# A graph layer on Trainium2: a mark on GpSimd ahead of every gather

## The chip, the cores and the metric

The kernel runs on one core of one Trainium2 chip. Its engines are called as in the profile: PE is TensorE (PEld its weight loads), DVE is VectorE, ACT is ScalarE, POOL is GpSimd and SP is SyncE. The metric is the device time of one execution in microseconds (us), and the lower the better. Times before are the median of three runs; the profile comes from one execution of its own, which has its own time.

## The reference

One layer of a graph transformer over 6250 nodes of 256 features in f32. It adds to the input x an attention over the edges (64 output features, 4 heads), a linear attention over all nodes, and then a mixture of experts (8 experts, the best 2 of them for each node). The part that this case is about is the attention over the edges:

```python
xn = _layernorm(x)
h = xn @ W                                 # 6250 x 64
el = h @ Wl.T;  er = h @ Wr.T              # 6250 x 4 heads each
e = exp(leaky_relu(el[src] + er[dst], 0.2))          # one row for each edge
rowsum = segment_sum(e, src, 6250)
w = e / maximum(rowsum, 1e-12)[src]
heads = [segment_sum(w[:, hd:hd+1] * h[dst], src, 6250) for hd in range(4)]
gnn = elu(stack(heads, axis=1) + b).reshape(6250, 256)
x = x + gnn + linear_attention(xn)
x = x + experts(_layernorm(x))
```

There are 206,250 edges: 100,000 in both directions and a loop on every node. They come sorted by dst, and the sums run over src, so the kernel sorts them by src. For every edge it needs the row of its dst node: `er` (4 numbers) and `h` (64 numbers).

## The kernel before, in words

**Tiles.** The 6250 nodes are 49 tiles of 128. First come the projections (`project`), and beside them the first pass of the sort (`sort_batch`), which drops every edge into a grid by pairs of src tiles. `project` also stores `table` in the chip's memory: one row of 69 f32 for each node, with `er`, `h` and a one.

**A block's edges.** `pack(q)` (L835) takes the pair q of src tiles, places its edges into 36 columns of 128 for each tile (35 of them used), and leaves two things: `dst_x` (L907, three buffers), the row numbers in `table`, and `loc` (L916), the place of each edge's src node in its tile. For each tile of the pair it then calls `gather`.

**The gather.** `gather` (L924) takes the buffer `xe` (three of them), 128 partitions by 35 columns by 69 f32, and issues 35 indirect DMAs from POOL (L927), one for each column: 128 rows of `table` chosen by one column of `dst_x`. 49 blocks of 35 gathers are 1715. They run on eight DMA semaphores in turn, so that a gather carries a wait for the one eight ahead of it. The first gather of a block waits besides for `dst_x` (DVE) and for the free `xe` buffer, which is free when the sums of the block three ahead of it (PE, `a_ps` at L996) have read it. From the first gather on POOL has no other work.

**What reads them.** `look(b, k)` (L935) builds the one-hot matrix `oh` of block b (L939), transposes it on PE (`t_ps`, L952), copies it with ACT (`ohT`, L956) and multiplies it with `elw` to give each edge its src part of the weight (`e_ps`, L964). `weights` (L971) adds up the three parts (L973), adds the gathered `er` (L977: the first reader of `xe`), takes the leaky relu and ACT's exponential, and puts the result in a PSUM bank. `sums` (L984) multiplies `oh` by the weights (`ohw`, L989, DVE) and sums the rows of `xe` on PE (`a_ps`, L996), with one matmul for each column. `xe` is the operand that is loaded as weights there, 65 columns wide, and the heads come out by `heads` (L789).

**The order.** The loop over blocks runs in program order, with `look` for the next block and `pack` for a pair two ahead put between the four steps of `sums`. Each step also runs a piece of other work with `some_more`: first the linear attention (`attention`, L543), then the experts of tiles that are done (`finish_steps`, L629; its matmuls are L739 and L755). Within an engine the instructions are in the order in which they were written; the engines meet through semaphores that the framework adds from the reads and writes of tiles. The loads and stores of x and of the output are issued from SP, and the gathers alone from POOL.

Of the kernel before, what the change touches and what calls it, by code (L numbers as in the profile page):

```python
# [34 lines left out]
def tile_gps_layer(  # L35
# [22 lines left out]
    nc = tc.nc  # L58
# [776 lines left out]
    def pack(q):  # L835
# [78 lines left out]
        for u in range(min(U, NT - q * U)):  # L914

            loc = gw.tile([P, GC, S, 2], BF16, name="loc", bufs=5)  # L916
            for i in range(S):
                nc.vector.scalar_tensor_tensor(
                    loc[:, :, i], lo[:, u, i * CS:i * CS + GC, None].to_broadcast([P, GC, 2]),
                    float(-u * P), lack[:, :, i], op0=OP.add, op1=OP.subtract,  # L920
                )
            ready[q * U + u] = (gather(dst_x[:, u * CW:u * CW + CPT]), loc)

    def gather(dst_x):  # L924
        xe = gw.tile([P, CPT, TW], F32, name="xe", bufs=3)
        for c in range(CPT):
            nc.gpsimd.indirect_dma_start(  # L927
                out=xe[:, c, :],
                out_offset=None,
                in_=table,  # L930
                in_offset=bass.IndirectOffsetOnAxis(ap=dst_x[:, c:c + 1], axis=0),
            )
        return xe

    def look(b, k):  # L935
# [252 lines left out]
```

## Time and profile before

| what | value |
|---|---|
| median of 3 runs | 4406.96 us (4391.23 to 4422.44) |
| profiled execution | 4420.71 us, of it span 4418.9 us |
| mean clock granted to TensorE | 0.694 |
| busy: PE / PEld | 2317.2 us / 1665.5 us |
| busy: DVE / ACT | 1975.3 us / 710.3 us |
| busy: POOL | 1678.3 us, of it gathers (L927) 1630.0 us in 1715 |
| software DMA queue (q0) | 54880 packets, 60.70 MB |

The span is the time between the first and the last instruction of the profiled execution, and 1.8 us lie around it. "Busy" is the time in which an engine works on an instruction; waits, semaphore instructions and the issuing of DMAs are not in it, apart from the gathers[...]. A line such as `L927` is a line of the kernel. In the profile's groups the columns are: line, engine, operation, output <- inputs, count; busy time and mean ns of one; idle time of the engine ahead of them, and what ended most of it. "remote" or "another core or an unknown queue" means that the profile found nothing that released the instruction. A list of durations such as `938/944/947` is the least, the median and the largest in ns. POOLq is the sequencer of POOL: the semaphore instructions stand under it.

The first gather starts at 459.9 us and the last at 4255.4 us. The gathers come in bursts of 35, one for each block.

### The profile page before, as it was taken

Reading aid. Unit: us, or ns where it says so; the run is one execution under the profiler, and the core shown is the slowest. Engines: PE = TensorE matmul, PEld = TensorE weight load, DVE = VectorE, ACT = ScalarE, POOL = GpSimd, SP = SyncE. Lnnn points to the kernel's source line nnn. Section 1 sums busy time; section 2 is a strip of 40 time slices with the busy share of each in tenths; the row PEclk is TensorE's granted clock in tenths of the full one; section 3 lists DMA queues with packets and bytes.
Section 4 is the critical chain, followed back from the end, with each engine's and each line's share of the span. In section 5 each row is a group of like instructions: output and inputs, shape, how many; then the busy total and the mean of one; then the engine's idle time right before and its main releaser. Section 6 shows DMA issues by size and latency. Waiting matters only on the chain.

```text
span 4418.9 us, 39444 instructions
## 1 busy us (share of the span) xinstructions
PE 2317.2 (52%) x15347; PEld 1665.5 (38%) x15347; DVE 1975.3 (45%) x4111; ACT 710.3 (16%) x1465; POOL 1678.3 (38%) x1779
## 2 busy tenths in 40 slices
PE   7876234333436554574645463464364463553658
PEld 4544123223324433352533342343243242342446
DVE  7889425443543443352543343244144253333443
ACT  4543001011101111111111110110110110110123
POOL 1001653445452433514343523523524435344220
PEclk8766556656657776696877675686686586685779
DMA  1120111111130101101100101100101101011010
GB/s 56 32 23 1 32 21 33 36 36 40 30 75 12 28 13 20 26 17 17 25 17 19 26 10 19 28 11 18 26 12 26 18 17 24 15 21 22 12 18 8
DMA packets 106677, 103.92 MB, mean 24 GB/s; under 512 B 42726, under 2 KB 78788, under 8 KB 106484
## 3 DMA queue, kind: packets, MB, share of 16 engines
q0 software_dynamic: 54880, 60.70, 8.0%
q1 hardware_dynamic: 49908, 39.75, 3.2%
q8 instruction: 122, 2.00, 0.2%
q10 hardware_dynamic: 1696, 0.89, 0.1%
q14 instruction: 71, 0.58, 0.0%
HBM read 86.57 MB, written 14.65 MB: 23 GB/s over the span
## 4 chain that ended last, share of the span: by engine, by line
another core or an unknown queue 37%; PE 24%; DVE 15%; issue 10%; ACT 4%; POOL 1%; DMA 0%; DVEq 0%; ACTq 0%; POOLq 0%
PE a_ps L996 8%; PE h_ps L739 6%; PE y_ps L755 6%; DVE rc L889 4%; DVE ohp L894 4%; DVE ohc L882 2%; PE y_ps L730 1%; POOL xe L927 1%; PE y_ps L679 1%; DVE ohw L989 1%; ACT ohT L956 1%; ACT hT L747 1%; DVE inc L853 1%; ACT L747 1%
## 5 line engine op out<-in xcount | busy, mean ns | idle before, releaser
L927 POOL DMA_INDIRECT xe<-table,dst_x x1715 | 1630.0, 950 | 2266.2 <-PE a_ps L996 1566.6
L996 PE MATMUL a_ps<-ohw,xe 128*65 128x128 f32 x4410 | 627.8, 298 | 302.3 <-issue 223.0
L996 PEld LDWEIGHTS a_ps<-ohw,xe 128*65 128x65 f32 x4410 | 563.4, 154 | 360.6 <-issue 262.7
L989 DVE TENSOR_TENSOR ohw<-oh,bank 128x1280 f32<-128x1280 bf16 x196 | 323.6, 1652 | 597.4 <-remote 514.3
L739 PE MATMUL h_ps<-tokT,w1s 128*128 128x512 f32 (+2 forms) x896 | 454.0, 625 | 79.5 <-ACT hT L747 58.4
L755 PE MATMUL y_ps<-w2s,hT 128*128 128x256 f32 x1568 | 438.8, 418 | 76.3 <-issue 71.6
L899 PE MATMUL s_ps<-rc,ohp 128*128 128x144 f16 x2525 | 267.4, 282 | 255.0 <-DVE ohp L894 202.9
L759 DVE SCALAR_TENSOR_TENSOR x<-y_ps,comb,x 128x256 f32<-128x256 f32 x392 | 189.6, 484 | 416.6 <-PE y_ps L755 295.6
L755 PEld LDWEIGHTS y_ps<-w2s,hT 128*128 128x128 f32 x1568 | 309.8, 208 | 172.4 <-issue 116.8
L964 PE MATMUL e_ps<-elw,ohT 128*128 128x48 bf16 x588 | 35.6, 198 | 623.7 <-ACT ohT L956 594.5
L899 PEld LDWEIGHTS <-ohp 128*128 128x128 f16 x2525 | 233.1, 125 | 319.9 <-DVE ohp L894 249.0
L747 ACT ACTIVATE hT<-h_ps,b1s 128x512 f32<-128x512 f32 (+2 forms) x224 | 142.0, 634 | 885.0 <-PE h_ps L739 404.6
L964 PEld LDWEIGHTS <-ohT 128*128 128x128 bf16 x588 | 28.7, 105 | 657.6 <-ACT ohT L956 614.7
L889 DVE TENSOR_TENSOR rc<-ohc,bank 128x1152 f16<-128x1152 f16 (+1 forms) x350 | 227.7, 695 | 57.5 <-remote 49.6
L956 ACT COPY ohT<-t_ps 128x768 bf16<-128x768 bf16 x98 | 78.2, 798 | 1070.0 <-remote 858.6
L739 PEld LDWEIGHTS h_ps<-tokT,w1s 128*128 128x128 f32 x896 | 172.6, 217 | 187.0 <-issue 95.3
L731 DVE TENSOR_TENSOR x<-x,y_ps 128x256 f32<-128x256 f32 x49 | 20.6, 421 | 404.0 <-PE y_ps L730 384.7
L894 DVE TENSOR_TENSOR ohp<-to,bank 128x2048 f16<-128x2048 f16 (+1 forms) x175 | 195.4, 1116 | 0.0
L853 DVE TENSOR_TENSOR_SCAN inc<-ones,t_ps 128x404 f32<-128x404 f32 x50 | 49.7, 993 | 284.4 <-remote 222.5
L567 PE MATMUL y_ps<-cw,qT 128*128 128x256 f32 x98 | 49.4, 599 | 203.7 <-ACT qT L565 89.2
L730 PE MATMUL y_ps<-b2s,cTs 8*128 8x256 f32 x98 | 55.4, 663 | 134.0 <-ACT cTs L728 134.0
L567 PEld LDWEIGHTS y_ps<-cw,qT 128*128 128x128 f32 x98 | 21.9, 273 | 272.5 <-ACT qT L565 161.9
(266 smaller groups left out, 2756.9 us busy)
## 6 DMA issues: line engine op xcount, KB each, us to landing
xe<-table,dst_x POOLq DMA_INDIRECT x1715
xt<-in_x_dram SPq DMA_DIRECT2D x24, 512.0 KB
base_y<-xt SPq DMA_DIRECT2D x12, 512.0 KB
yt<-base_y SPq DMA_DIRECT2D x11, 512.0 KB
out_dram<-x SPq DMA_DIRECT2D x11, 512.0 KB
w1s<-in_L_ffn_w_dram SPq DMA_DIRECT2D x8, 256.0 KB
w2s<-in_L_ffn_w_dram SPq DMA_DIRECT2D x8, 256.0 KB
table<-tab SPq DMA_DIRECT2D x12, 138.0 KB
```

Source lines behind the costliest of these rows:

```text
L730: nc.tensor.matmul(yb, lhsT=cTs, rhs=b2s, start=True, stop=True)
L739: nc.tensor.matmul(h_ps[:, :w], lhsT=w1s[:, e, c, f * P:(f + 1) * P], rhs=held["tokT"][:, c, :w], start=(c == 0), stop=(c == DC - 1),)
L747: nc.scalar.activation(held[e][:, f, :w], h_ps[:, :w], AF.Gelu, bias=b1s[:, k:k + 1])
L755: nc.tensor.matmul(y_ps, lhsT=held[e][:, f, j * P:(j + 1) * P], rhs=w2s[:, e, f, :], start=(f == 0), stop=(f == FC - 1),)
L759: nc.vector.scalar_tensor_tensor(x2[:, j, :], y_ps, held["comb"][:, j, e:e + 1], x2[:, j, :], op0=OP.mult, op1=OP.add,)
L889: nc.vector.tensor_tensor(pairs(rc[:, :m, i, :]), pairs(ohc[:, :m]), twos(edges_q[:, t0:t0 + m, i, :], U * CW // 2), op=OP.mult,)
L894: nc.vector.tensor_tensor(pairs(ohp[:, :m]), twos(to[:, 1, t0:t0 + m], P // 2), iota_2.to_broadcast([P, m, P // 2, 2]), op=OP.is_equal,)
L899: nc.tensor.matmul(flat(s_ps), lhsT=ohp[:, t - t0, :], rhs=flat(rc[:, t - t0]), start=(t == 0), stop=(t == NBT - 1),)
L927: nc.gpsimd.indirect_dma_start(out=xe[:, c, :], out_offset=None, in_=table, in_offset=bass.IndirectOffsetOnAxis(ap=dst_x[:, c:c + 1], axis=0),
L956: nc.scalar.copy(ohT, t_ps)
L989: nc.vector.tensor_tensor(ohw[:, :n], oh[:, g0:g1, i, None, :].to_broadcast([P, n, H, SN]), ew_s[:, c0:c0 + n, :, None].to_broadcast([P, n ...
L996: nc.tensor.matmul(a_ps[:, i].rearrange("f h n -> f (h n)"), lhsT=xe[:, c, H:], rhs=ohw[:, c - c0].rearrange("p h n -> p (h n)"), start=(c ...
```

## The change

`gather` calls a new function `in_turn` for each of its DMAs. It puts an instruction that does nothing (`nop`, the mark) on POOL ahead of the gather. Two dependences without a semaphore keep the order: the mark behind the gather before, and the gather behind its own mark. A dependence with a semaphore makes the gather wait for the mark of the gather ahead of it, across blocks too. The very first gather has no such wait. In the built program each mark is one semaphore instruction on POOL that raises a semaphore of POOL's own. A gather waits for one semaphore: where it was the DMA semaphore of the gather eight ahead, it is now the mark's, and the wait for the DMA semaphore is a semaphore instruction of its own between the mark and the gather. POOL has 1927 instructions before and 5334 after, with 1717 DMAs in both.

```diff
@@ -921,15 +921,36 @@
+    issued = []
+    marks = []
+
+    def behind(ins, other, by):
+        tc.add_manual_dep(
+            ins.ins, other.ins.name, mybir.DependencyInfo(by, mybir.DependencyReason.DATA)
+        )
+
+    def in_turn(issue):
+
+
+        mark = nc.gpsimd.nop()
+        if issued:
+            behind(mark, issued[-1], mybir.DependencyClass.NoSync)
+        row = issue()
+        behind(row, mark, mybir.DependencyClass.NoSync)
+        if marks:
+            behind(row, marks[-1], mybir.DependencyClass.Sync)
+        marks.append(mark)
+        issued.append(row)
+
     def gather(dst_x):
         xe = gw.tile([P, CPT, TW], F32, name="xe", bufs=3)
         for c in range(CPT):
-            nc.gpsimd.indirect_dma_start(
+            in_turn(lambda: nc.gpsimd.indirect_dma_start(
                 out=xe[:, c, :],
                 out_offset=None,
                 in_=table,
                 in_offset=bass.IndirectOffsetOnAxis(ap=dst_x[:, c:c + 1], axis=0),
-            )
+            ))
         return xe
```

## The prediction

> **What bounds the kernel now.** I read the page's busy row first, then the chain that ended last, then the groups of the changed line, and last the trace around one block's gathers, by windows.
>
> ```profile
> PE 2317.2 (52%) x15347; PEld 1665.5 (38%) x15347; DVE 1975.3 (45%) x4111; ACT 710.3 (16%) x1465; POOL 1678.3 (38%) x1779
> another core or an unknown queue 37%; PE 24%; DVE 15%; issue 10%; ACT 4%; POOL 1%; DMA 0%; DVEq 0%; ACTq 0%; POOLq 0%
> L927 POOL DMA_INDIRECT xe<-table,dst_x x1715 | 1630.0, 950 | 2266.2 <-PE a_ps L996 1566.6
> L956 ACT COPY ohT<-t_ps 128x768 bf16<-128x768 bf16 x98 | 78.2, 798 | 1070.0 <-remote 858.6
> ```
>
> No engine is full, and 37% of the chain is put down to something the profile can't name: 0.37 x 4418.9 = 1635 us. POOL's share of the chain is 1%, so the gathers look like no bound. The windows say otherwise. These are 48 us before a burst of 35 gathers (one block's) and the 43 us from 6.5 us after its start:
>
> ```profile
> core 0: us, PE busy (x) PEld busy (x) DVE busy (x) ACT busy (x) POOL busy (x), PEclk, DMA share, GB/s
> 2570.00:2618.00 48.00, 45.09 (x283) 31.57 (x281) 40.85 (x86) 9.99 (x15) 0.00 (x0) 1.00 0.00 1
> 2625.00:2668.00 43.00, 5.18 (x34) 3.70 (x33) 3.99 (x4) 0.06 (x1) 28.00 (x30) 0.59 0.16 26
> ```
>
> PE goes from 45 busy us in 48 to 5 in 43. The chain over the same place, and the gathers there:
>
> ```profile
> 2620.13 0.69 ACT hT L747
> 2620.81 47.10 another core or an unknown queue
> 2667.94 0.81 ACT ohT L956
> ```
>
> ```profile
> L927 POOL DMA_INDIRECT xe<-table,dst_x x35: 938/944/947, 2618.5 to 2660.9; - x35
> L927 POOLq EVENT_SEMAPHORE  x2: 43/38638/77232, 2537.8 to 2654.6; - x2
>   issue: 10.1, 33
> ```
>
> The last gather ends at 2661.84; ACT resumes 6.1 us later. The trace has the semaphore updates of PE's matmuls that were issued ahead of the stall arriving one by one through the burst. So while POOL issues gathers, PE's completions come late and everything that hangs on them stands. Why, the trace doesn't show. The same picture is at most of the 49 bursts, with ACT waits of 47.0 to 47.1 us at 1461, 1626, 2288, 2942, 3260, 3577, 3895 and 4215. As data the gathers are early (block 14's end at 1502.2, their reader, the add into z at L977, runs at 1622.4); only block 0's are waited for directly. Hence the rule for the sum: **a burst that gets longer by d moves the end by about d**, for some 42 of the 49 bursts; 42 is the count in this row, where POOL found PE's release before it:
>
> ```profile
> POOL xe L927 <- PE a_ps L996: 1566.6, 42, 82.9
> ACT ohT L956 <- remote: 858.6, 34, 47.1
> ```
>
> Here page and trace disagree. The Trainium skill, SBUF — State Buffer, section "SBUF: two separate sides", says engine ports and DMA ports are disjoint, so that a DMA and a compute operation don't slow each other. By that rule a burst longer by 5 us costs nothing (the data has 36 to 120 us to spare); by the windows above it costs about 42 x 5 = 210 us. I take the windows.
>
> **The change, part by part.** The instruction order on PE, DVE, ACT, SP and POOL stays as it was; there are 1715 gathers before and after, the same DMAs. Added on POOL's queue are 3407 semaphore instructions: 1715 marks, and about 1692 separate waits. A gather of before carries one wait, that the gather eight ahead of it has landed. After, it carries the wait for the mark, and the wait for the landing stands as an instruction of its own ahead of it.
>
> The gather itself: 0.944 us (median of the row) and a constant gap of 0.30 us (10.1 us of issue over 33), so a cadence of 1.249 us and 35 x 1.249 - 0.30 = 43.4 us a burst. The first eight gathers of the program carry no landing wait and have the same gap, so a satisfied wait on a gather costs nothing there. The new wait is for the mark ahead of the *previous* gather, which POOL's sequencer has executed before it ever reaches this gather: always satisfied, **0**. Behind a gather on POOL stand only later gathers; their readers are L977 and L996's weight loads.
>
> The marks and separate waits: the nearest row is the EVENT_SEMAPHORE of L927, 43 ns when satisfied; the one place with two in a row (458.894 and 458.981) has them 87 ns apart. Two for each gather: 87 to 174 ns of the sequencer's time, 150 to 300 us over the kernel if nothing hid it. The cover is that the sequencer runs ahead. In the burst above, the semaphore instruction of the *next* block is at 2654.6, just before gather 29 of 35 starts (2654.65): six gathers were already handed over and waiting. So the sequencer made 35 gathers in 2654.65 - 2618.47 = 36.2 us, at most 1.03 us each, and since it meets the start of a gather to 0.1 us it was being held by a full queue and needs less. Even 1.03 + 0.174 = 1.21 us is under the cadence of 1.249. The ends: **0** (all hidden) and 0.174 x 35 x 42 = **256 us** (all exposed). I take 0, because the row shows the sequencer six ahead, and keep 256 for the range.
>
> A rule speaks against this. Advanced Engine Details and Errata, section "Network/Comms", gives 50 to 100 ns for reading a semaphore from a sequencer on trn2: 100 to 200 ns for two a gather, an estimate of 42 x 35 x (0.1 to 0.2) = 147 to 294 us if it were on the path. The trace has 43 to 87 ns and the run-ahead; by these the sum is 0.
>
> The moved wait: the landing wait now holds the sequencer, not the queue. Packets start 1.64 us after a gather's issue and have landed 2.1 to 2.7 us after it; the gather eight later is due 8 x 1.249 = 9.99 us after. 7.3 us to spare, **0**. The run-ahead may shrink; one gather ahead is enough.
>
> At the first gather of a block, the mark and waits are passed while the sequencer still waits for dst_x (the 77.2 us instruction at 2537.8), and the gather then starts 0.26 us after PE's release, as before. If they came after the release instead: 42 x 0.087 to 0.174 = 4 to 7 us. I take **+4**. Code: the skill's Runtime: NRT & Kernel Launch, section "Instruction fetch mechanics", has 256 instructions in 16 KiB, so 64 B each; 3407 are 218 KB, an estimate of 27 more packets of the size that the instruction queue q14 shows (0.58 MB in 71, 8 KB). Ends: 0 and 27 x 2.1 us (a gather's landing as the nearest transfer) = 57 us. Before, POOL's 1927 instructions needed some 15 such packets and no gap of 0.30 inside a burst shows one; two exposed is my choice, **+4**.
>
> **Sum** against the profiled execution: 4420.7 + 4 + 4 = 4429. That execution lies 14 us over the median of the runs shown, 4407; on the median's footing the forecast is **4415**. A measurement of this kernel tells about 1% from no change: 4363 to 4451.
>
> **Rivals.**
> A, slower: the sequencer isn't far enough ahead once it has three instructions for one. It decides from the point where mark, wait and gather together take over 1.249 us of the sequencer, or where marks fill queue places so that the run-ahead runs dry. For: at most 1.03 us is known today, so as little as 0.05 us more than I count puts it over; 30 ns a gather is already 35 x 42 x 0.03 = 44 us, 1%. Against: the alignment to a full queue. Price: one instruction exposed 0.087 x 35 x 42 = 128 us, 4543; both 256 us, 4671.
>
> B, slower by code: pages exposed one after another, 57 us, 4472. Against: fetching ahead was invisible so far; for: three times as many in the same bursts.
>
> C, faster: what delays PE in the bursts is eased. For: 1635 us of the chain are unexplained; the stall starts 4 to 12 us into a burst, when the sequencer is at the gathers whose wait names one of the same burst, and the change takes that wait off the gathers. Against: the stall outlasts the last gather by 6 us, when no gather waits, and PE's matmuls at L899 in the first bursts, which wait for no gather, are late too. A tenth of 1635 us is 164 us: 4251.
>
> That the change does nothing that counts is the forecast itself, as its wait is always satisfied.
>
> **How the numbers follow.** Forecast (hidden) 0.40, A 0.26, B 0.10, C 0.24. So faster by over 1% 0.24, within 1% 0.40, slower 0.36. The forecast's own range is 4385 to 4440. The range is 4290 to 4600: it holds the forecast, B, A with one instruction exposed, and the smaller half of C; the far half of C (0.12) and A with both exposed (0.08) are left out.
>
> **What would show it.** Right: gathers of 0.944 us with a gap of 0.30, bursts of 43.4 us, some 3450 EVENT_SEMAPHORE on the gathers' lines, ACT waits of 47 us unchanged, the chain's unknown share at 37%. A: the gap between gathers grows to 0.39 or 0.48 and the ACT waits to 50 or 53 us, the next block's semaphore instruction moves to the burst's end. B: single gaps of about 2 us, up to 27 of them. C: the same cadence, yet PE busy well over 5 us in the 43, and shorter ACT waits. Wrong altogether if the gathers themselves change their 0.944 us.

## The result, and the profile after

The changed kernel takes **4538.93 us** (median of 4 runs, 4530.64 to 4543.47) against 4402.57 us of the kernel before in the same comparison: a ratio of 1.031, 95% interval 1.0277 to 1.0343. It is slower by 3%, some 136 us. The profiled execution has a span of 4537.6 us against 4418.9, which is 118.7 us more at nearly the same granted clock (0.691 against 0.694).

From the page of the changed kernel: the busy row, the chain's shares, the gathers' group, and the queue that brings instructions.

```profile
PE 2378.6 (52%) x15347; PEld 1700.8 (37%) x15347; DVE 1974.3 (44%) x4111; ACT 709.8 (16%) x1465; POOL 1681.0 (37%) x1779
...
another core or an unknown queue 35%; PE 22%; DVE 15%; issue 13%; ACT 3%; POOL 2%; DMA 1%; POOLq 1%; DVEq 0%; ACTq 0%
...
L948 POOL DMA_INDIRECT xe<-table,dst_x x1715 | 1632.5, 952 | 2386.3 <-POOLq L935 1593.1
```

```profile
q14 instruction: 98, 0.80, 0.1%
```

The gathers are busy as long as before (1632.5 us against 1630.0). q14 brings 98 packets instead of 71, exactly the 27 that the prediction counted. The lines of the gathers and of the marks by themselves, with the least, median and largest duration in ns:

```profile
L948 POOLq EVENT_SEMAPHORE  x1744: 2/17/119346, 335.2 to 4371.4; - x194
L948 POOL DMA_INDIRECT xe<-table,dst_x x1715: 939/947/1928, 455.6 to 4373.7; - x191
```

```profile
L935 POOLq EVENT_SEMAPHORE  x1714: 2/17/1397, 11.5 to 4368.6; - x191
```

The two lines have 3458 semaphore instructions, and they take POOL's sequencer 17 ns in the median. Some 50 of them are the waits at the head of a block, which stood there before (51 on L927). So POOL does nearly what was expected of it: its gap between two gathers is still 0.305 us in the median.

Where are the 119 us? Worked out from the starts and ends of the gathers: the 49 bursts last 2173.0 us in all, before 2137.7 (+35.3); the time between bursts is 1746.0 us, before 1658.8 (+87.2); what lies ahead of the first burst and behind the last is 4 us less. **Three quarters of the loss lie where no gather runs.** One pair of bursts shows how. These are windows of before, a burst (44 us) and the stretch up to the next burst:

```profile
3325.00:3369.00 44.00, 8.40 (x70) 6.35 (x68) 7.90 (x15) 1.38 (x2) 33.01 (x35) 0.63 0.16 32
3369.00:3407.00 38.00, 20.33 (x164) 17.78 (x164) 30.72 (x58) 2.39 (x6) 0.42 (x1) 0.58 0.02 2
```

And the same two of after (columns: window, length, busy us of PE, PE's weight loads, DVE, ACT and POOL with counts, clock, share of the DMA engines, GB/s):

```profile
3413.00:3457.00 44.00, 5.39 (x52) 5.15 (x52) 2.52 (x6) 0.21 (x1) 32.95 (x35) 0.59 0.15 28
3457.00:3501.00 44.00, 23.53 (x178) 19.54 (x178) 35.38 (x67) 3.15 (x7) 0.37 (x1) 0.56 0.02 1
```

The burst is the same for POOL: 35 gathers, 33 us busy. PE gets 52 matmuls through in it instead of 70, and DVE does 6 operations instead of 15. The work that did not fit comes after the burst, and the stretch grows from 38 to 44 us. Over all bursts, 3817 of PE's matmuls start inside them before, and 3394 after. Counted by the gather beside which they start, the loss is at one place: beside the sixth to tenth gather of a burst PE starts 1103 matmuls before and 560 after. Ahead of that it is 1691 and 1647, and from the eleventh gather on there are even more after (1187 against 1023).

The granted clock hardly moved: over the bursts 0.643 before and 0.639 after, between them 0.730 and 0.724. But the matmuls moved within it. From the first burst on, 3689 of them start while the clock is at half, before 3335, and PE's busy time is 61 us more for the same 15347 matmuls. How much of the loss comes in this way and how much by later starts is not shown.

The other 35 us are single gaps in some bursts: 30 gaps over 0.4 us, together 32.6 us over the usual one. The gathers at the end of the seventh burst:

```profile
897.13 0.94 POOL L948 DMA_INDIRECT xe<-table,dst_x  x1 [0.33 <-issue]
899.94 0.95 POOL L948 DMA_INDIRECT xe<-table,dst_x  x1 [1.86 <-DMA xe<-table,dst_x]
902.04 0.95 POOL L948 DMA_INDIRECT xe<-table,dst_x  x1 [1.16 <-issue]
904.84 0.95 POOL L948 DMA_INDIRECT xe<-table,dst_x  x1 [1.85 <-DMA xe<-table,dst_x]
```

In the trace the marks and waits around them take 0.69 to 0.71 us each instead of 17 ns, and some twice that. 574 of POOL's semaphore instructions are that slow, half of them behind position 28 of a burst and hardly any ahead of 20 outside the first four bursts. PE's semaphore updates in the bursts mostly arrive at multiples of about 0.70 us, before as after (2.80, 2.13, 3.52, 5.60 us in the burst at 2618 of before). Of 236 steps of over 0.35 us between such updates, from 7 us into a burst on, 202 lie within 0.08 us of a multiple before, and 111 of 131 after. Two engines with the same step of 0.7 us suggested the first theory: in a burst, the sequencers of all engines get something in turns of 0.7 us.

### The profile page after: what moved, and what is told of

Same layout as the page of the kernel before. It is cut to its first block, busy times and chain, and to the rows that moved or that the text cites. A ratio compares the mean times of both kernels' runs of the same rounds, so it can differ in the third digit from the quotient of the medians.

```text
span 4537.6 us, 42851 instructions
## 1 busy us (share of the span) xinstructions
PE 2378.6 (52%) x15347; PEld 1700.8 (37%) x15347; DVE 1974.3 (44%) x4111; ACT 709.8 (16%) x1465; POOL 1681.0 (37%) x1779
## 4 chain that ended last, share of the span: by engine, by line
another core or an unknown queue 35%; PE 22%; DVE 15%; issue 13%; ACT 3%; POOL 2%; DMA 1%; POOLq 1%; DVEq 0%; ACTq 0%
PE a_ps L1017 7%; PE h_ps L739 6%; PE y_ps L755 6%; DVE rc L889 4%; DVE ohp L894 3%; DVE ohc L882 2%; POOL xe L948 2%; PE y_ps L730 1%; DVE ohw L1010 1%; DVE inc L853 1%; ACT ohT L977 1%; DMA xe<-table,dst_x 1%; ACT hT L747 1%; DVE x L759 1%
## 5 line engine op out<-in xcount | busy, mean ns | idle before, releaser
L948 POOL DMA_INDIRECT xe<-table,dst_x x1715 | 1632.5, 952 | 2386.3 <-POOLq L935 1593.1
L1017 PE MATMUL a_ps<-ohw,xe 128*65 128x128 f32 x4410 | 666.7, 307 | 366.0 <-issue 334.3
L1017 PEld LDWEIGHTS a_ps<-ohw,xe 128*65 128x65 f32 x4410 | 591.5, 159 | 442.5 <-issue 395.3
L739 PE MATMUL h_ps<-tokT,w1s 128*128 128x512 f32 (+2 forms) x896 | 476.2, 647 | 179.5 <-ACT hT L747 110.4
L1010 DVE TENSOR_TENSOR ohw<-oh,bank 128x1280 f32<-128x1280 bf16 x196 | 322.8, 1647 | 550.8 <-remote 528.1
L882 DVE TENSOR_TENSOR ohc<-to,bank 128x1152 f16<-128x1152 f16 (+1 forms) x175 | 120.0, 686 | 0.4 <-ACT to L871 0.4
L426 DVE TENSOR_TENSOR ohp<-rank,iota_h 128x4096 f16<-128x4096 f16 (+1 forms) x51 | 115.7, 2269 | 2.8 <-ACT rank L419 2.6
```

The source lines that it names most:

```text
L739: nc.tensor.matmul(h_ps[:, :w], lhsT=w1s[:, e, c, f * P:(f + 1) * P], rhs=held["tokT"][:, c, :w], start=(c == 0), stop=(c == DC - 1),)
L882: nc.vector.tensor_tensor(pairs(ohc[:, :m]), twos(to[:, 0, t0:t0 + m], U * CW // 2), iota_2[:, :, :U * CW // 2].to_broadcast([P, m, U * CW ...
L948: in_turn(lambda: nc.gpsimd.indirect_dma_start(out=xe[:, c, :], out_offset=None, in_=table, in_offset=bass.IndirectOffsetOnAxis(ap=dst_x[: ...
L1010: nc.vector.tensor_tensor(ohw[:, :n], oh[:, g0:g1, i, None, :].to_broadcast([P, n, H, SN]), ew_s[:, c0:c0 + n, :, None].to_broadcast([P, n ...
L1017: nc.tensor.matmul(a_ps[:, i].rearrange("f h n -> f (h n)"), lhsT=xe[:, c, H:], rhs=ohw[:, c - c0].rearrange("p h n -> p (h n)"), start=(c ...
```

## The experiments

Each ratio is against runs of the kernel before on the same chip. Their medians differ by chip (4411.9 us for the first four, 4363.95 for the next four, 4408.99 for the last two), so the spans of different groups are not compared to one per cent.

**One of the two added instructions, or both without the moved wait.** The theories at the start were the turns, a store of instructions ahead of POOL's sequencer that runs out, and the landing wait that was moved from the gather's queue into the sequencer.

```diff
-        mark = nc.gpsimd.nop()
-        if issued:
-            behind(mark, issued[-1], NoSync)
+        if len(issued) < 8:
+            issued.append(issue())
+            return
+        wait = nc.gpsimd.nop()
+        behind(wait, issued[-1], NoSync)
+        behind(wait, issued[-8], Sync)
         row = issue()
-        behind(row, mark, NoSync)
-        if marks:
-            behind(row, marks[-1], Sync)
+        behind(row, wait, NoSync)
```

> One part alone: no marks. Ahead of each gather from the ninth on stands one semaphore instruction that waits for the landing of the gather eight ahead; the gather keeps its own landing wait, which is then always satisfied. One added instruction a gather instead of two. Theory 1 (turns: every semaphore instruction that POOL's sequencer executes in the late part of a burst takes 0.7 us that PE's instructions would have had): about half of the change's cost, +50 to +80 us, and some 0.7 us semaphore instructions late in the bursts. Theory 2 (a store of some 90 instructions ahead of POOL's sequencer that runs out: 35 x 3 = 105 is over it, 35 x 2 = 70 is not): 0 within 20 us, and no 0.7 us semaphore instruction. Theory 3 (the landing wait that was moved from the queue to the sequencer is the cost): all of it, +120 to +140 us.

Measured: 4488.77 us, ratio 1.018 (1.0145 to 1.0214), +77 us. The other part:

```diff
         mark = nc.gpsimd.nop()
         if issued:
             behind(mark, issued[-1], NoSync)
+        seen_it = nc.gpsimd.nop()
+        behind(seen_it, mark, Sync)
         row = issue()
-        behind(row, mark, NoSync)
-        if marks:
-            behind(row, marks[-1], Sync)
+        behind(row, seen_it, NoSync)
```

> The other part alone: ahead of each gather a mark and a semaphore instruction that waits for this mark; the landing wait stays on the gather as before. Two added instructions a gather, as in the change, none with a landing wait. Theory 1 (turns) and theory 2 (store of some 90 instructions): as the change, +110 to +150 us. Theory 3 (moved landing wait): 0 within 20 us.

Measured: 4523.63 us, ratio 1.0256 (1.0221 to 1.0291), +112 us. Without any moved landing wait most of the loss is there, so the third theory falls. One added instruction costs somewhat more than half of what two cost, which fits the turns. The store falls too: with one added instruction it should not have run out. One detail goes against the turns as I had put them: in the run with waits alone, not one of POOL's semaphore instructions took 0.7 us, and PE lost all the same (3601 matmuls in the bursts). It did not lose them where the change does, though: beside the sixth to tenth gather it starts 1038, nearly as many as before.

**Early or late in the burst.**

```diff
-            in_turn(lambda: nc.gpsimd.indirect_dma_start(
+            (in_turn if c < 20 else issue_it)(lambda: nc.gpsimd.indirect_dma_start(
```

> The change for the first 20 gathers of each block, the last 15 as before: 57% of the marks. Theory 1 (turns, counted late in the burst): 0 to +30 us. Theory 2: 20 x 3 + 15 = 75 instructions a burst, 0 within 20 us. A cost that is the same for each mark, wherever it stands: 0.57 x 136 = +78 us.

Measured: 4537.43 us, ratio 1.0292 (1.0255 to 1.0328), +126 us. With `c >= 20` instead:

> The change for the last 15 gathers of each block, the first 20 as before: 43% of the marks. Theory 1 (turns, counted late in the burst): +90 to +140 us, nearly the whole cost. Theory 2: 20 + 15 x 3 = 65 instructions a burst, 0 within 20 us. A cost that is the same for each mark: 0.43 x 136 = +58 us.

Measured: 4452.51 us, ratio 1.0103 (1.0066 to 1.014), +41 us. My expectation was the wrong way round. The early marks alone cost as much as all of them. They hardly slow POOL itself (18 slow semaphore instructions; 249 in the run with late ones), while PE's matmuls in the bursts fall to 3390, as after the change, and again beside the sixth to tenth gather (573; with the late marks 1088). So the slow instructions on POOL are a symptom and not the cost. With two added instructions a gather the loss is PE's, and it is taken early.

**The first ten only** (`c < 10`).

> The change for the first 10 gathers of each block only, half of what the run with the first 20 had (+126 us). A cost in proportion: +63 us. If PE loses by what POOL's sequencer takes in while PE still runs at speed, in the first 10 us of a burst: nearly all, +90 to +126 us. If the second ten made the cost: 0 to +30 us.

Measured: 4419.44 us against 4363.95, ratio 1.0138 (1.0104 to 1.0173), about +60 us by the ratio: in proportion. 957 added instructions in the first 10 gathers cost 60 us, and the 980 of the next 10 another 66 us (126 - 60). Where these 60 us lie is open. The trace has 3766 matmuls in the bursts, 1034 of them beside the sixth to tenth gather, nearly as many as before; and of the kernel before there is no trace from this chip to set the rest against.

**The instructions on another engine.** This tests whether the marks act through POOL at all.

```diff
+    def other_queue(ahead):
+        for _ in range(71):
+            nop = nc.sync.nop()
+            tc.add_manual_dep(nop.ins, ahead.ins.name, DependencyInfo(Sync, DATA))
+            ahead = nop
...
-                sums(k, oh, xe, a_ps)
+                last_mm = sums(k, oh, xe, a_ps)
+                if k == S - 1:
+                    other_queue(last_mm)
```

> The kernel before with no marks on POOL, and on SP's queue a chain of 71 semaphore instructions for each block, each waiting for the one ahead of it, that starts when PE has ended the block's sums, which is where a burst of gathers starts too. If what the added instructions take from PE in a burst is a turn in something that all engines' sequencers share: +70 to +140 us, and SP's instructions at 0.7 us in the bursts. If only POOL's own instructions count: within 25 us of before.

Measured: 4523.55 us against 4363.95, ratio 1.0371 (1.0338 to 1.0405). POOL's program is that of before, and the loss is even greater. The chain of one block in the burst from 2679.13 to 2722.51:

```profile
L937 SPq EVENT_SEMAPHORE  x68: 2/17/709, 2679.0 to 2707.3; - x68
```

68 instructions that need nothing but each other take 28.3 us. The last three chains of the same run start behind the last burst. One of them:

```profile
L937 SPq EVENT_SEMAPHORE  x70: 17/17/17, 4397.9 to 4402.8; - x70
```

That is 4.9 us for 70. Nor is it SP's own transfers that are held up: the loads that stand behind the chains (`yt`, L642) are issued 18 to 330 us ahead of their reader, as in the kernel before (20 to 320 us). The counter-test has chains of the same instructions outside the bursts, started by `pack`:

```diff
-                if k == S - 1:
-                    other_queue(last_mm)
...
+            if t0 == 0:
+                other_queue(first)      # first: the product ohc of pack, 141 nops
```

> The kernel before with the chain of semaphore instructions on SP's queue moved out of the bursts: 141 for each pair of blocks, the same number as 71 for each block, started by the first product of pack on DVE, some 30 us ahead of the next burst and at least 9 us after the last for nearly all pairs. At the 67 ns that one of the chain took outside bursts it lasts 9.5 us. If the cost of the chain that starts with the bursts (+3.7%) comes from the bursts: within 0.5% of before. If it comes from the instructions themselves, or from what SP's transfers wait for behind them: again +100 us or more.

Measured: 4420.87 us against 4408.99, ratio 1.0015 (1.0 to 1.003). The loss is gone but for 0.3% at most. 23 of the 25 chains lie wholly outside the bursts. One of them:

```profile
L939 SPq EVENT_SEMAPHORE  x140: 17/17/17, 2599.3 to 2609.2; - x140
```

140 instructions in 9.9 us, 71 ns each; in the burst they took 28.3 / 67 = 0.42 us each. So it is the burst that makes a sequencer's instruction expensive, on POOL and on SP alike, and with such instructions in the bursts PE gets less (3205 matmuls there).

**More of it.**

```diff
+        first = nc.gpsimd.nop()
+        if issued:
+            behind(first, issued[-1], NoSync)
         mark = nc.gpsimd.nop()
-        if issued:
-            behind(mark, issued[-1], NoSync)
+        behind(mark, first, Sync)
```

> The change with a second mark ahead of each gather, which the first mark waits for: three added semaphore instructions a gather (5,130 in all) instead of two. If each added instruction takes a turn from PE, the cost goes on with the count: 77 us for one and 136 us for two point to +190 to +210 us, with more and longer gaps inside the bursts. If the cost is settled by the wait on the mark alone: as the change, +125 to +145 us.

Measured: 4488.61 us against 4408.99, ratio 1.0162 (1.0102 to 1.0221), +71 us by the ratio. Neither expectation: three added instructions cost half of what two do. In the trace POOL's sequencer is now too slow for its own gathers:

```profile
2679.22 0.94 POOL L949 DMA_INDIRECT xe<-table,dst_x  x1 [1.51 <-issue]
2682.03 0.94 POOL L949 DMA_INDIRECT xe<-table,dst_x  x1 [1.87 <-POOLq L937]
2683.51 0.94 POOL L949 DMA_INDIRECT xe<-table,dst_x  x1 [0.53 <-POOLq L934]
```

222 such gaps make the bursts 217.3 us longer in all (2355.0 us), but the time between them shrinks to 1530.0 us, 128.8 less than before. PE starts 3766 matmuls inside the bursts, nearly as many as before. The early loss is greater still (403 beside the sixth to tenth gather), but beside the last 15 gathers PE starts 984 where it started 268 before and 348 after the change. It doesn't do so in the gaps themselves: in the 222 of them, 286 us, it starts 188 matmuls, fewer for each us than beside the gathers. So PE gets time back late in these bursts; that the gaps give it, with a delay, is a guess.

**What the bursts are worth, and whether they can be cut up.** First nearly all gathers out:

```diff
+    kept = []
     def gather(dst_x):
-        xe = gw.tile([P, CPT, TW], F32, name="xe", bufs=3)
+        if len(kept) == 3:
+            kept.append(kept.pop(0))
+            return kept[-1]
+        xe = gw.tile([P, CPT, TW], F32, name=f"xe{len(kept)}", bufs=1)
+        kept.append(xe)
```

> The kernel before, with gathers for the first three blocks only; blocks 3 to 48 read these rows again, so 46 x 35 gathers are left out. This gives the worth of all bursts together. If the bursts hold up PE, 46 stalls of some 35 us go: about 2800 to 3000 us. If they are hidden behind other work: within 3% of before.

Measured: 2637.08 us against 4363.95, ratio 0.6044 (0.602 to 0.6068), and the chain's first place goes from the unknown to PE:

```profile
PE 45%; DVE 27%; issue 6%; another core or an unknown queue 3%; ACT 3%; POOL 2%; DMA 0%; DVEq 0%; ACTq 0%; POOLq 0%
```

The 1610 gathers left out are worth 1727 us, 1.07 us each, of a cadence of 1.25 us. Its busy row:

```profile
PE 2081.7 (79%) x15347; PEld 1551.5 (59%) x15347; DVE 1963.4 (74%) x4111; ACT 711.5 (27%) x1465; POOL 149.6 (6%) x169
```

PE's busy time is 236 us less than before, at a granted clock of 0.832 instead of 0.694. Were all of that on the path and none of it the gathers' doing, 0.93 us a gather would be left, an estimate. As long as POOL gathers, the rest of the core gets little done: over the 49 bursts of before PE is busy for 642 of 2138 us, between them for 1194 of 1659.

Then all gathers, in pieces of 8 or 9 with each step of the sums two blocks ahead:

```diff
+            if b + 2 < NT:
+                rows[b + 2] = gather(ready[b + 2][0])     # the tile alone
             for k in range(S):
-                sums(k, oh, xe, a_ps)
+                step = sums(k, oh, xe, a_ps)              # step: its product on DVE
+                if b + 2 < NT:
+                    columns(b + 2, CPT * k // S, CPT * (k + 1) // S, step)
```

> The kernel before, with a block's 35 gathers spread over the four steps of a block's sums (8 or 9 with each step, the first of them waiting for this step's product on DVE), instead of one burst of 35. The number of gathers, waits and marks is as before. If PE is slowed only once a burst has lasted some microseconds (its stall starts 4 to 12 us into a burst), pieces of 11 us leave most of it out: 3000 to 4000 us. If every gather costs PE its share wherever it stands: within 1% of before, 4370 to 4450 us. If the gathers come too late for their block: above 4450 us.

Measured: 4262.01 us against 4363.95, ratio 0.9764 (0.973 to 0.9798). It is the fastest kernel with the whole computation here, faster than both, but the large gain that a stall with a starting time would have given is not there: a gather costs PE about its share in a piece of 9 as in a burst of 35. Where its 2.4% come from was not tried.

The runs in one table. "Added" counts instructions of the built program; bursts and the time between them are us from the trace; matmuls are those of PE that start from a burst's first gather to 1.5 us behind its last, and in the last column those that start from the sixth gather to the eleventh. The run with the first 10 and the chain inside the bursts were profiled on the chip with the quickest runs of before (4363.95 us), so their times in the trace can't be set against the first row to one per cent.

| run | added | ratio | bursts | between | matmuls in bursts | beside gathers 6 to 10 |
|---|---|---|---|---|---|---|
| before | 0 | 1 | 2137.7 | 1658.8 | 3817 | 1103 |
| the change | 3407 on POOL | 1.031 | 2173.0 | 1746.0 | 3394 | 560 |
| waits alone | 1693 on POOL | 1.018 | 2141.3 | 1720.7 | 3601 | 1038 |
| marks, landing wait unmoved | 3409 on POOL | 1.026 | 2157.9 | 1758.6 | 3329 | 512 |
| first 20 gathers | 1937 on POOL | 1.029 | 2146.6 | 1770.5 | 3390 | 573 |
| first 10 gathers | 957 on POOL | 1.014 | 2139.9 | 1653.1 | 3766 | 1034 |
| last 15 gathers | 1468 on POOL | 1.010 | 2137.7 | 1680.1 | 3738 | 1088 |
| a second mark | 5122 on POOL | 1.016 | 2355.0 | 1530.0 | 3766 | 403 |
| chain on SP, in bursts | 71 a block | 1.037 | 2138.6 | 1767.7 | 3205 | 381 |
| chain on SP, outside | 141 a pair | 1.002 | 2137.8 | 1666.2 | 3805 | 1087 |

## Why the prediction was right or wrong

The likeliest case, no change at 4415 us, was wrong. The range held, and the slower side had 0.36, but by luck: what had widened the range up to 4600 us was rival A, and its mechanism is not what the runs show.

**The bound was read rightly.** That the bursts, with 1% of the chain on POOL, hold up the kernel was taken from the windows. Leaving the gathers out took 1727 us away; the prediction had 1635 us in the unknown share. The block that it showed, PE busy for 5 us in 43 (12%), is far under the mean of all bursts, 30%. Where it says that page and trace disagree, it goes too far. The rule of the Trainium skill, SBUF — State Buffer, section "SBUF: two separate sides", is about ports, and the instructions' own time agrees with it: DVE is busy for 1975.3 us with all gathers and for 1963.4 us with 105 of them, ACT for 710.3 and 711.5 us. What the gathers hold up is when instructions start and when their completions arrive.

**The step that failed is "the marks and separate waits: 0, because the sequencer is six ahead".** The cover it named was real: POOL's gathers kept their gap of 0.305 us, and POOL lost only the 35 us of single gaps. But the sum asked only who waits on POOL. The price was paid by PE, none of whose instructions waits for a mark: 423 matmuls fewer in the bursts, 87 us more between them. The window that showed PE at 5 us in 43 beside the burst was the hint that the burst draws on something that PE needs too; the prediction used it to price longer bursts and did not ask what else draws on it. The row of 43 and 87 ns that I took for the price of a semaphore instruction was no guide: in the run with the chain on SP one cost 71 ns outside a burst and 0.42 us in it. The 50 to 100 ns for reading a semaphore from a sequencer (the Trainium skill, Advanced Engine Details and Errata, section "Network/Comms") agree with the 71 ns outside the bursts and fall short of the 0.42 us in them.

**The rule "a burst that gets longer by d moves the end by about d" failed as well.** With the second mark, 217 us of longer bursts moved the end by about 71 us. A burst that is longer by gaps does not cost its length; one that is longer by gathers was not tried, but each gather was worth 1.07 us of its 1.25.

**Rival A** gave 4543 us for one instruction exposed, 4 us from the measured time, and its size was right by chance. It wanted the gap between gathers at 0.39 us; the gap stayed. What it said of a run-ahead that runs dry did occur, in 30 gaps worth 32.6 us, and in 222 gaps with the second mark. **Rival B**: its 27 packets came, but the trace's fetches don't lie at the gaps, and there are 0.7 us semaphore instructions at the gaps. The run with SP's chain outside the bursts brings 99 packets on the same queue and lost nothing that counts, so the packets by themselves are not the price. **Rival C** had the sign wrong; its evidence, a wait on the gathers that names one of the same burst, was met by the run with waits alone, where the gathers' own waits are always satisfied and PE still lost.

What is **open**: what it is that the sequencers seem to share while POOL gathers. It shows on POOL, PE and SP alike, in steps of 0.7 us, from the first microseconds of a burst (SP's chain goes at 0.15 us an instruction in the first 4 us and at 0.33 us in the next four), and outside the bursts SP's chain shows nothing of it. Instructions that have nothing to do with semaphores were not tried on an idle queue, so it isn't settled whether the supply of instructions or the access to semaphores is what runs short. Nor can these runs tell whether the profiler's own record of each instruction has a part in it: every time here comes with a span and a granted clock from such a record. Why the late marks cost less, and where the runs with one added instruction a gather and with the first 10 lose their time, is open too.

## What to carry to other kernels

Before calling an added instruction free because its own engine is ahead, look at what the other engines do in the same stretch: if PE slows while POOL gathers, semaphore instructions in that stretch can cost PE time, on POOL's queue or on another one's. Put bookkeeping (marks, chains, separate waits) outside the gathers: chains of as many semaphore instructions on SP cost 0.3% at most there and 3.7% inside. And a stall put down to "an unknown queue" can be priced by leaving its suspect out once, with an eye on the granted clock, which may change too.

## What the runs showed of the hardware

A semaphore instruction on an otherwise idle queue took 71 ns in a chain, and 0.42 us in a chain that ran beside indirect DMAs issued from POOL. Single ones take 0.7 us there (877 of SP's 3044), and most of PE's completions come in steps of the same size. Each indirect DMA of 128 rows of 276 bytes cost the kernel about 1.07 us, what the higher granted clock gave included, though the busy time of DVE and ACT stayed the same. An added semaphore instruction on POOL in that stretch cost some 40 ns of the kernel's time in the change (136 us / 3407), and between 14 ns (71 us / 5122, with the second mark) and 63 ns (60 us / 957, in the first 10 gathers) in the other runs, though POOL's own gathers kept their cadence in most of them.
